# Two transformer layers on one core: order of row loads, weight fetches and leftover expert tiles in layer 0

## The chip, the cores and the metric

The kernel runs on one core of a Trainium2 chip. The metric is device time in microseconds for one execution of the whole program. Every engine (TensorE, VectorE, ScalarE, GpSimd, SyncE) runs its own list of instructions in order; semaphores tie the lists together. TensorE is called PE in the profile, VectorE DVE, ScalarE ACT, GpSimd POOL and SyncE SP.

## What is computed

Input x has 8 sequences of 512 tokens with 256 features, all in float32. Two layers follow one another; each is an attention part and an expert part, with a modulated layer norm before each and a gate after each. Only layer 0 is concerned here. Cut to what matters:

```python
# attention of layer 0: a delta rule, a serial scan over the 512 tokens
q = l2norm(silu(x @ Wq.T)); k = l2norm(silu(x @ Wk.T)); v = silu(x @ Wv.T)
beta = sigmoid(x @ Wbeta.T)                      # one per head, 16 heads of 16
def step(M, (q_t, k_t, v_t, b_t)):
    out_t = einsum('bnh,bnhd->bnd', q_t, M)
    delta = v_t - einsum('bnhd,bnd->bnh', M, k_t)
    return M + b_t * einsum('bnh,bnd->bnhd', k_t, delta), out_t
# experts of layer 0: each token goes to one of 8 experts
top = argmax(x @ gate_w.T + gate_b + expert_bias)
y   = relu(x @ w1[top] + b1[top]) @ w2[top] + b2[top]        # 256 -> 1024 -> 256
```

Layer 1 is a causal softmax attention with a relative bias, and a mixture of 8 dense experts.

## The kernel before, in words

The 512 tokens are cut into four chunks of 128 (`NT = 4`). For each chunk i three things are done.

**Front** (`front`): the tokens are loaded, normed (`stats`, L498 to L509 on ScalarE; `normal`, L525 and L526 on VectorE), turned (`turn`, L140 to L145), projected to q, k, v (`project`, L543 to L557), scaled (`roots`, `scales`, L668 to L676) and laid out by head (`heads`). `stats` of the last pair of sequences also clears the slot rows of its chunk in DRAM (L514, 1920 KB).

**Scan** (`scan`, L741 to L756): 128 steps of four VectorE instructions, each step needing the state of the step before.

**Follow** (`follow`): attention from the scan's deltas (`attend`; `deltas` L775, `turn` L786, `scores` L812, `weigh` L873, `project` L894 and L898, `rest` L929 to L934), routing (`route`), and the experts (`experts`). `attend` also loads the chunk's tokens once more for the residual (`tokens`, L768) on SyncE's queue, into eight buffers. Routing ends in the ranks' products on TensorE (L1074 to L1079); VectorE works out from them each token's slot and each slot tile's expert (L1087 to L1120, the last being `idx`). A chunk's 8 x 128 tokens are put by expert into 15 slot tiles of 128 rows (`NSLOT`), each tile belonging to one expert. Eight indirect DMAs on GpSimd's queue scatter the tokens to their rows in DRAM (`scatter`, L1126). Then for each slot tile j:

- its rows are loaded on SyncE's queue (L1162, two buffers), turned on TensorE (L1165) and copied by ScalarE (L1169); the code calls this `turn(j)`;
- first half: 32 products with w1 (L1190) and eight relus (L1199), which read the bias in the same weight tile;
- second half: 16 products with w2 (L1209), a copy (L1214), the bias add on GpSimd (L1215, which reads the second weight tile), and the store to DRAM on GpSimd's queue (L1216).

The weights of slot j come in two parts, fetch(j, 0) with w1 and b1 (1.05 MB) and fetch(j, 1) with w2 and b2 (1.18 MB), both indirect DMAs on GpSimd's queue (L1145). Each part has two buffers, so fetch(j, part) waits until slot j - 2 has done with its tile; the count runs on from one chunk to the next. After the slots, gathers (L1227) bring the results back to token order.

**What sets the order.** Each piece of front and follow has a place, a number. While chunk i + 1 is scanned, the pieces of chunk i's follow, of chunk i + 2's front and what was left of chunk i - 1's follow are sorted by place, and each is written out once the scan has come to the step of that number. A VectorE instruction of a piece is tied behind that scan step. On the other engines the place gives only priority: a scheduler orders each engine's list by priority and by when it expects an instruction's inputs. `tc.issue_after(ins)` ties every instruction written in its block that runs on the engine of `ins` behind `ins`. After the last scan there are no steps: the rest of chunk 2's slots, the attention of chunk 3 and its routing are written in order of place, then chunk 3's slots.

In `follow`, `late` says how many slots run during the scan, from place 68 on at `pace` places a slot; the others go to `starts` in the stretch after (during the next scan for chunks 0 and 1, after the last scan for chunk 2).

```python
            fetch(0, 0)
            with tc.issue_after(issued["fetch"]):
                scatter()
            with tc.issue_after(issued["scatter"]):
                fetch(0, 1)
                fetch(1, 0)
            yield
            turn(0)
```

Before the change GpSimd thus issues one fetch, the eight scatters, and then two fetches.

Of the kernel before, what the change touches and what calls it, by code (L numbers as in the profile page):

```python
# [19 lines left out]
P = 128  # L20
# [5 lines left out]
NT = S // P  # L26
# [37 lines left out]
def tile_two_layers(ctx: ExitStack, tc: tile.TileContext, t: dict, out: bass.AP):  # L64
    nc = tc.nc
# [212 lines left out]
    with ExitStack() as l0:  # L278
# [478 lines left out]

        def attend(i, qk, V, x1, norms):
# [6 lines left out]
            def tokens():  # L765
                for b in range(B):
                    x1.append(fp.tile([P, D], F32, tag="x1", name=f"x1_{i}_{b}", bufs=8))
                    nc.sync.dma_start(x1[b], t["x"][b, i * P : (i + 1) * P, :])  # L768
# [121 lines left out]
            def project(b):  # L890
# [6 lines left out]
                for g in range(2):  # L897
                    nc.tensor.matmul(  # L898
                        py[:, D : D + 1], sqT[:, g, :], cst[:, C_ONES : C_ONES + 1],
                        start=(g == 0), stop=(g == 1),  # L900
                    )
# [44 lines left out]
            pieces = [(0, deltas), (1, tokens)]  # L946
# [16 lines left out]


        DEPTH = (3, 3, 1, 1)

        issued = {}

        def route(i, h, norms):
# [31 lines left out]
            for half in range(2):  # L1001
# [3 lines left out]
                for n in range(5):  # L1005
                    b = 4 * half + n
# [72 lines left out]
            nc.tensor.matmul(  # L1079
# [3 lines left out]
            )  # L1083
# [51 lines left out]
        def experts(i, slot, idx, scatter):  # L1135
# [37 lines left out]
            fetch(0, 0)  # L1173
            with tc.issue_after(issued["fetch"]):
                scatter()
            with tc.issue_after(issued["scatter"]):
                fetch(0, 1)
                fetch(1, 0)
# [55 lines left out]
            if i == NT - 1:  # L1234
                rows = [w1["rows"][:, b * D : (b + 1) * D] for b in range(B)]
# [31 lines left out]
        def follow(i, qk, V):  # L1267


            x1, norms = [], []  # L1270
            _, pieces = attend(i, qk, V, x1, norms)
# [13 lines left out]
            def on():  # L1285
                next(work["experts"])

            pieces += [(34, begin), (42, more), (51, more), (57, more), (60, more), (62, settle)]

            late, pace, starts = {  # L1290
                NT - 1: (0, 4, [10 * j for j in range(NSLOT)]),
                NT - 2: (14, 4.2, [43]),
                NT - 3: (11, 4.6, [8, 22, 37, 47]),
            }.get(i, (11, 4.6, [8, 22, 37, 47]))
            rest = []
            for j in range(NSLOT):
                for half in range(2):
                    if j < late:
                        pieces.append((68 + pace * (j + half / 2), on))
                    else:  # L1300
                        rest.append((starts[j - late] + 3 * half, on))
# [52 lines left out]
        parts, pieces, later = front(0, 0)  # L1354
        run(pieces)
        rest, gathers = [], []
# [404 lines left out]
```

## Time and profile before

| | |
|---|---|
| median of 3 runs | 2216.25 us (2212.28 to 2221.45) |
| the profiled execution | 2215.8 us, its span 2214.1 us |
| scans 0 to 3 | 52 to 299, 299 to 570, 570 to 846, 846 to 1098 us |
| VectorE busy | 1580.6 us (71%) |
| TensorE busy | 1718.3 us (78%) |
| weight fetches | 120, on GpSimd's queue |
| slot rows loaded | 60 x 128 KB, on SyncE's queue |
| end of chunk 3's slots | 1344 us |
| TensorE's granted clock, mean | 0.874 |

All times are counted from the start of the span. A line of a timeline has the start, the time taken (both us), the engine, the line of the kernel, the operation, what is written and read, and a count; in brackets, how long the engine had been idle and what ended that. `PEld` is TensorE's loading of weights, `SPq` an issue on SyncE's queue. In the list of waits: who waited for whom, the total in us, how often, the longest. A line of windows gives the stretch, its length, the busy time of PE, PEld, DVE, ACT and POOL with instruction counts, TensorE's granted clock, the busy share of the 16 DMA engines and GB/s.

### The profile page before, as it was taken

The numbers are of one execution on the slowest core, as the hardware profiler recorded it, in microseconds if no ns is written. First come the engines' busy times: TensorE is split into PE (matmuls) and PEld (weight loads), VectorE is DVE, ScalarE is ACT, GpSimd is POOL, SyncE is SP. The second block draws the span as 40 slices with busy tenths as digits, with TensorE's granted clock in tenths as the row PEclk, the third lists the DMA queues.
The fourth block names the chain that finished last, engine by engine and source line by source line (L and its number), as shares of the span: only waits on it lengthen the run. The fifth ranks groups of instructions, "written<-read, shape, count | busy, mean of one in ns | idle before, by whom it ended". The sixth has DMA issues, their size and how long they took to land. (4 is left out here: it accounts for less than half of the span.)

```text
span 2214.1 us, 32513 instructions
## 1 busy us (share of the span) xinstructions
PE 1718.3 (78%) x10906; PEld 1196.4 (54%) x10906; DVE 1580.6 (71%) x4523; ACT 1081.1 (49%) x2674; POOL 642.1 (29%) x920
## 2 busy tenths in 40 slices
PE   5342056479686796839995898999999999999988
PEld 4221035259574695728874786555555555555544
DVE  5999998969989699899753004677676666676754
ACT  4253035555366553623342336886666574747421
POOL 1313013355254553543463643010111101010210
PEclk8666566689897898969997999999999999999998
DMA  5110000358103582128765883000101010000101
GB/s 165 49 50 5 0 1 11 99 209 313 33 13 108 198 311 72 38 90 303 234 110 153 272 275 72 1 20 8 27 13 25 13 22 13 22 20 6 23 17 12
DMA packets 88630, 189.58 MB, mean 86 GB/s; under 512 B 13688, under 2 KB 67104, under 8 KB 75664
## 3 DMA queue, kind: packets, MB, share of 16 engines
q0 software_dynamic: 33696, 137.43, 19.3%
q1 hardware_dynamic: 54768, 50.09, 7.9%
q8 instruction: 86, 1.41, 0.3%
q14 instruction: 80, 0.66, 0.1%
HBM read 175.10 MB, written 36.93 MB: 96 GB/s over the span
## 5 line engine op out<-in xcount | busy, mean ns | idle before, releaser
L1433 ACT ACTIVATE pr<-sc,low 128x384 f32<-128x384 f32 (+3 forms) x512 | 255.6, 556 | 196.3 <-DVE low L1428 193.2
L1428 DVE CUSTOM_DVE_ANT_0 sc<-ps,strips 128x384 f32<-128x384 f32 (+3 forms) x512 | 225.6, 486 | 87.2 <-PE ps L1419 55.6
L1190 PE MATMUL ps<-hTs,w 128*128 128x128 f32 x1920 | 239.4, 286 | 14.0 <-DMA w<-in_wrows,idx 9.0
L1190 PEld LDWEIGHTS ps<-hTs,w 128*128 128x128 f32 x1920 | 235.5, 201 | 21.4 <-issue 11.6
L745 DVE TENSOR_REDUCE state<-terms 128x16 f32<-128x272 f32 x512 | 227.3, 444 | 15.6
L756 DVE TENSOR_TENSOR state<-state,upd 128x256 f32<-128x256 f32 x511 | 222.2, 435 | 14.9
L1590 PE MATMUL ps<-ew,hTd 128*128 128x512 f32 x512 | 232.6, 608 | 0.0
L1209 PE MATMUL ps<-w,act 128*128 128x256 f32 x960 | 223.7, 387 | 6.5 <-DMA w<-in_wrows,idx 4.0
L741 DVE TENSOR_TENSOR terms<-state,K 128x256 f32<-128x256 f32 x512 | 216.3, 422 | 14.9
L751 DVE TENSOR_TENSOR upd<-K,state 128x256 f32<-128x256 f32 x511 | 214.4, 420 | 16.1
L1199 ACT ACTIVATE act<-ps,w 128x128 f32<-128x128 f32 x480 | 137.3, 370 | 135.4 <-PE ps L1190 122.2
L1445 PE MATMUL ps<-cst,pr 128*128 128x128 f32 x1280 | 189.9, 292 | 15.3 <-DVE low L1428 12.0
L1209 PEld LDWEIGHTS ps<-w,act 128*128 128x128 f32 x960 | 182.0, 195 | 31.4 <-issue 4.0
L1595 DVE SCALAR_TENSOR_TENSOR accd<-ps,wtd,accd 128x256 f32<-128x256 f32 x256 | 123.7, 483 | 100.7 <-PE ps L1590 86.6
L1445 PEld LDWEIGHTS ps<-cst,pr 128*128 128x128 f32 x1280 | 147.2, 147 | 84.8 <-DVE low L1428 24.1
L1599 POOL TENSOR_TENSOR accd<-accd,bc_g 128x256 f32<-128x256 f32 x28 | 20.4, 728 | 545.6 <-DVE accd L1595 545.6
L1145 POOL DMA_INDIRECT w<-in_wrows,idx x120 | 124.2, 1035 | 184.1 <-ACT act L1199 58.8
L1590 PEld LDWEIGHTS ps<-ew,hTd 128*128 128x128 f32 x512 | 96.3, 193 | 120.5 <-issue 106.4
L1419 PE MATMUL ps<-kT,qTc 32*128 32x128 f32 (+3 forms) x1024 | 132.1, 491 | 4.4 <-DVE low L1428 2.6
L1454 DVE COPY prT<-ps 128x512 f32<-128x512 f32 (+3 forms) x256 | 117.0, 484 | 8.9 <-PE ps L1445 8.5
L1452 ACT COPY prT<-ps 128x512 f32<-128x512 f32 (+3 forms) x256 | 98.9, 414 | 7.2 <-PE ps L1445 6.6
L1165 PE MATMUL ps<-cst,hslot 128*128 128x128 f32 x120 | 24.7, 290 | 98.2 <-DMA hslot<-hs 71.3
(296 smaller groups left out, 2956.3 us busy)
## 6 DMA issues: line engine op xcount, KB each, us to landing
hs<-zero SPq DMA_DIRECT2D x4, 1920.0 KB
hslot<-hs SPq DMA_DIRECT2D x60, 128.0 KB
ys<-ysb POOLq DMA_DIRECT2D x60, 128.0 KB
x<-in_x SPq DMA_DIRECT2D x32, 128.0 KB
strips<-strip_d SPq DMA_DIRECT2D x16, 256.0 KB
out<-accd POOLq DMA_DIRECT2D x32, 128.0 KB
wm<-in_wmod SPq DMA_DIRECT2D x4, 768.0 KB
xt<-in_x SPq DMA_DIRECT2D x12, 256.0 KB
```

What stands on the lines that cost most here:

```text
L741: nc.vector.tensor_mul(term[:, :, :HD], M, K[:, s, :].unsqueeze(1).to_broadcast([P, HD, HD]))
L745: nc.vector.tensor_reduce(delta, term, AX.X, ALU.add)
L751: nc.vector.tensor_mul(upd, K[:, s, :].unsqueeze(2).to_broadcast([P, HD, HD]), delta.unsqueeze(1).to_broadcast([P, HD, HD]),)
L756: yield nc.vector.tensor_sub(M, M, upd).ins
L1190: nc.tensor.matmul(ph[:, q * P : (q + 1) * P], w[:, k * FF + f * P : k * FF + (f + 1) * P], hT[:, k, :], start=(k == 0), stop=(k == 1),)
L1199: nc.scalar.activation(act[:, f, :], ph[:, q * P : (q + 1) * P], AF.Relu, bias=w[:, 2 * FF + f : 2 * FF + f + 1],)
L1209: nc.tensor.matmul(py[:, :D], act[:, f, :], w[:, f * D : (f + 1) * D], start=(f == 0), stop=(f == NFC - 1),)
L1419: made = nc.tensor.matmul(pscs[r][:, :W], qT[rows, g, o, i * P : (i + 1) * P], kT[rows, g, :W], start=True, stop=True,)
L1428: nc.vector.tensor_tensor_reduce(out=sc[:, :W], in0=pscs[r][:, :W], in1=strips[:, n, S - W :], scale=1.0, scalar=3.0e38, op0=ALU.add, op1= ...
L1433: nc.scalar.activation(pr, sc[:, :W], AF.Exp, bias=low, scale=-1.0)
L1445: nc.tensor.transpose(pt[:, (i - j) * P : (i - j + 1) * P], prs[r, i][:, j * P : (j + 1) * P], ident,)
L1590: nc.tensor.matmul(pe, hT[0][:, k, cols], ew[:, k, e : e + 2, :], start=(k == 0), stop=(k == 1),)
```

## The change

Four edits, all in layer 0.

1. `tokens`: the loads are tied behind the slot row that was issued last when the piece is written (`issued["rows"]`), if there is one. They are on the same queue.
2. `experts`: fetch(0, 0), fetch(0, 1) and fetch(1, 0) come first, then the eight scatters.
3. The first slot's place goes from 68 to 70. Chunk 2 runs 12 slots, not 14, during the last scan.
4. Slots left over: those at a place below 43 are written as before; one at 43 has its TensorE instructions tied behind the attention's last product written so far (L898), those at 61 behind the ranks' last product (L1079). For chunks 0 and 1 the four left go to 8, 22, 40, 61 (before: 8, 22, 37, 47); for chunk 2 three go to 43, 61 and 61.4 (before: one at 43).

```diff
             def tokens():
                 for b in range(B):
                     x1.append(fp.tile([P, D], F32, tag="x1", name=f"x1_{i}_{b}", bufs=8))
-                    nc.sync.dma_start(x1[b], t["x"][b, i * P : (i + 1) * P, :])
+                    with ExitStack() as order:
+                        if "rows" in issued:
+                            order.enter_context(tc.issue_after(issued["rows"]))
+                        nc.sync.dma_start(x1[b], t["x"][b, i * P : (i + 1) * P, :])
...
-            fetch(0, 0)
+            for j, part in ((0, 0), (0, 1), (1, 0)):
+                fetch(j, part)
             with tc.issue_after(issued["fetch"]):
                 scatter()
-            with tc.issue_after(issued["scatter"]):
-                fetch(0, 1)
-                fetch(1, 0)
             yield
             turn(0)
...
+            def behind(what):
+                with tc.issue_after(issued[what]):
+                    on()
+
             pieces += [(34, begin), (42, more), (51, more), (57, more), (60, more), (62, settle)]
 
             late, pace, starts = {
                 NT - 1: (0, 4, [10 * j for j in range(NSLOT)]),
-                NT - 2: (14, 4.2, [43]),
-                NT - 3: (11, 4.6, [8, 22, 37, 47]),
-            }.get(i, (11, 4.6, [8, 22, 37, 47]))
+                NT - 2: (12, 4.3, [43, 61, 61.4]),
+            }.get(i, (11, 4.6, [8, 22, 40, 61]))
             rest = []
             for j in range(NSLOT):
                 for half in range(2):
                     if j < late:
-                        pieces.append((68 + pace * (j + half / 2), on))
+                        pieces.append((70 + pace * (j + half / 2), on))
+                        continue
+                    place = starts[j - late]
+                    if i == NT - 1:
+                        rest.append((place + 3 * half, on))
+                    elif place < 43:
+                        rest.append((place + 3 * half, on))
                     else:
-                        rest.append((starts[j - late] + 3 * half, on))
+                        what = "ranks" if place > 60 else "attention"
+                        rest.append((place + 0.2 * half, lambda what=what: behind(what)))
```

The rest of the diff records `issued["attention"]` at L898 and `issued["ranks"]` at L1079, and moves `issued` and `DEPTH` up. Here `on` runs the next half of a slot, `begin` and `more` the stages of routing, `settle` the last stage with the fetches and scatters.

More of the change, by code (lines that the diff above doesn't have):

```diff
@@ L756, in scan @@
                 yield nc.vector.tensor_sub(M, M, upd).ins
+        DEPTH = (3, 3, 1, 1)
+        issued = {}
         def attend(i, qk, V, x1, norms):
@@ L897, in project @@
                 for g in range(2):
-                    nc.tensor.matmul(
+                    issued["attention"] = nc.tensor.matmul(
                         py[:, D : D + 1], sqT[:, g, :], cst[:, C_ONES : C_ONES + 1],
                         start=(g == 0), stop=(g == 1),
-                    )
+                    ).ins
                 h = b // 4
@@ L962, in attend @@
             return got, pieces
-        DEPTH = (3, 3, 1, 1)
-        issued = {}
         def route(i, h, norms):
@@ L1078, in route @@
             )
-            nc.tensor.matmul(
+            issued["ranks"] = nc.tensor.matmul(
                 pr[:, B * NE : B * NE + NE], count,
@@ L1082, in route @@
                 start=True, stop=True,
-            )
+            ).ins
             yield
```

## The prediction

> **What bounds the kernel now.** I read the page first: busy times and the 40 slices (55.4 us each), then the waits of VectorE, then the timelines of the engines around the two places where VectorE stands still.
>
> ```profile
> PE 1718.3 (78%) x10906; PEld 1196.4 (54%) x10906; DVE 1580.6 (71%) x4523; ACT 1081.1 (49%) x2674; POOL 642.1 (29%) x920
> DVE  5999998969989699899753004677676666676754
> ```
>
> No engine bounds the whole. VectorE is at 9 from slice 2 to slice 19: there run the four scans of layer 0, one instruction after the other, from 52 to 1098 us. Then come a stretch in which TensorE works off the last chunk (1098 to 1344 us) and layer 1, which the change does not touch. So the change is worth what it takes out of VectorE's stalls before 1098 us, plus what it takes out of the stretch up to 1344 us.
>
> The waits of VectorE within scans 1 and 2 (297 to 846 us):
>
> ```profile
> DVE rsa L525 <- ACT sda L509: 39.8, 4, 19.1
> ```
>
> Two of those four are 18.1 us (to 474.6) and 19.1 us (to 751.0); everything else in the scans is under 3 us each. Around the second, ScalarE, then SyncE's queue:
>
> ```profile
> 717.50 0.26 ACT L669 ACTIVATE beta<-beta 128x64 f32<-128x64 f32 x1
> 732.98 0.37 ACT L1169 COPY hTs<-ps 128x256 f32<-128x256 f32 x1 [15.22 <-PE ps L1165]
> ...
> 745.08 0.41 ACT L498 ACTIVATE ps<-xt 128x256 f32<-128x256 f32 x1
> ...
> 750.65 0.29 ACT L509 ACTIVATE sda<-mva,cst 128x2 f32<-128x2 f32 x1
> ```
> ```profile
> 715.86 5.39 SPq L768 DMA_DIRECT2D x<-in_x  x7
> 721.87 0.58 SPq L1162 DMA_DIRECT2D hslot<-hs  x2
> ```
> ```profile
> 712.00:722.00 10.00, 0.00 (x0) 0.00 (x0) 9.38 (x25) 5.69 (x9) 8.01 (x10) 0.61 0.94 327
> 722.00:732.00 10.00, 0.00 (x0) 0.00 (x0) 9.14 (x22) 0.00 (x0) 1.53 (x5) 0.50 0.85 326
> ```
>
> ScalarE stands 15.2 us at the copy of slot 0's turned rows; the statistics of the next chunk (L498, L509), which need nothing of slot 0, are queued behind that copy, and VectorE's L525 waits for them. The rows were asked for at 721.9 and reached TensorE at 732.3, 10.4 us later; seven token loads stand ahead of them in SyncE's queue. The last two columns of the windows: the 16 DMA engines are 94 and 85% busy, TensorE does nothing.
>
> The stretch after the scans:
>
> ```profile
> 1094.38 3.62 PE L1209 MATMUL ps<-w,act 128*128 128x256 f32 x16
> 1103.21 5.44 PE L1190 MATMUL ps<-hTs,w 128*128 128x128 f32 x32 [5.21 <-DMA w<-in_wrows,idx]
> ...
> 1112.16 1.96 PE L775 MATMUL ps<-cst,V 128*128 128x128 f32 x16
> ```
> ```profile
> 1188.10 0.54 PE L1079 MATMUL ps<-cst,count 64*128 64x8 f32 x2
> ...
> 1191.88 1.10 POOL L1145 DMA_INDIRECT w<-in_wrows,idx  x1 [9.86 <-DVE idx L1120]
> 1193.64 1.04 POOL L1126 DMA_INDIRECT hs<-h_last,slot  x1 [0.66 <-issue]
> ...
> 1202.66 0.97 POOL L1126 DMA_INDIRECT hs<-h_last,slot  x1 [0.30 <-issue]
> 1203.94 1.04 POOL L1145 DMA_INDIRECT w<-in_wrows,idx  x1 [0.30 <-issue]
> ...
> 1211.53 0.69 PE L1165 MATMUL ps<-cst,hslot 128*128 128x128 f32 x2 [22.89 <-DMA hslot<-hs]
> ```
>
> The scan's last copy (L747) ends at 1098.1, but chunk 2's slot 13 holds TensorE until 1112.2 before the last attention (L775) begins. From the ranks' products (end 1188.6) to slot 0's rows (1211.5) TensorE is empty for 22.9 us. Then 15 slots take 132 us.
>
> **What the Trainium skill says.** "DMA: Bandwidth & Descriptors", sections "Queues, rings and completion order" and "Issuing engines are not separate DMA queues": each DMA engine takes a ring in order and goes round-robin between rings, and all issuing engines share the same 16. The trace agrees: the rows take 10.4 us from issue to use behind tokens and weights, 8.0 in scan 3 (992.3 to 1000.3), 5.6 in the last stretch with no tokens (1205.9 to 1211.5). "Perfetto Trace Analysis", section "Sequencer Loop": an engine's queued instruction waits for its semaphores; here the 15.2 us with ready statistics behind it. "TensorE: Matmul & The Clock Gate", section "What's actually happening": an idle TensorE falls to half clock. The windows agree (0.50), and slot 0's 32 products take 5.4 to 6.0 us after a bubble, 3.7 otherwise.
>
> **The change part by part.**
>
> *Tokens behind rows.* 8 loads of 128 KB leave the space ahead of and beside slot 0's rows, in scans 1, 2 and 3. They go behind the slot row last issued (chunk 1's to about 553 us, chunk 3's to about 1080, ahead of the strips at 1087.7) and are first needed 25 steps into the next attention: nothing is late. The 1 MB beside the weights of slots 12 and 13 is covered by the 7 us that TensorE has to spare before 1098; gone, it would cost some 3 us. The rows save the 1.05 MB; the rows' own time goes from 10.4 towards 5.6, so 3 to 5 us.
>
> *Three fetches ahead of the eight scatters.* GpSimd issues a fetch in 1.3 us (1203.94, 1205.29), so the scatters start 2.6 us later. Where DMA is full (scans 1 and 2, 0.94 to 1.00 of 16 engines, the clearing of the next chunk's slot rows, 1.92 MB issued at 702.8, among it), their data also queue behind 1.18 + 1.05 MB, which at 327 GB/s is 6.8 us; 5.4 at the 0.41 MB per us that the packets reach at best. The scatters' packets ended about 717.3; so 722.7, 2 us to the semaphore, and about 4 us for the rows (only one fetch beside them): 728.7 against 732.3. **Minus 3 us** in scan 2; the same sum for scan 1 (scatters' packets end 442.5, rows 456.1) gives 2 to 3. In scan 3, with no clearing in the way, +2.6 and -2.5 cancel: 1000 us as before.
>
> *What this does to the stalls.* The ScalarE chain from rows to L509 is 18.7 us (732.3 to 751.0), of which 6.0 are slot 0's products at half clock. It moves with the rows: **-3 in each of scans 1 and 2, -6**. If the shift from place 68 to 70 and the later rows put the statistics ahead of the copy, the stall goes nearly whole (a rival below). I take -6, ends 0 and -30.
>
> *Slots moved within scans 2 and 3.* Slot 14 goes from place 47 to behind the ranks. Its 7.3 us of products (3.7 + 3.6) go where TensorE was idle (972.3 to 1000.3 in scan 3), and no longer delay the attention's last projection: VectorE's 0.9 us waits at 663, 666, 940, 942 us may go, **-2**. In scan 2 they lie ahead of the front's projections 2 and 3 (702 to 712), which may make L525 at 715 wait up to 4 us; that only takes from the longer stall after it, since that one ends by the rows. Cover gone, it costs 4.
>
> *Twelve slots, not fourteen, in scan 3.* Slot 11 ends at 1090.8, before the scan (1098.1), so the last attention starts then and not at 1112.2: **-14.0**. Slot 12 takes slot 14's old place (1172.0 to 1179.2, while ScalarE and VectorE finish the rows): 0. The ranks end at R = 1174.6.
>
> *Slots 13 and 14 behind the ranks.* 14.6 us of products in a bubble of 22.9: hidden themselves. But weights have two buffers per part. Before, fetch(0,0) went at R + 3.2, when the indices were there. Now it waits for slot 13's activations (R + 3.7 + 1.5 = 5.2), fetch(0,1) for slot 13's bias add (R + 7.4 + 2.5 = 9.9), fetch(1,0) for slot 14's activations (R + 11 + 1.5 = 12.5), and the scatters queue behind it: R + 14.1, not R + 5.0. **+9.1**, plus 1.6 if slot 14's bias add and store (0.7 + 0.6 and gaps) go between. Against it, the rows have one fetch beside them, not three: 5.6 becomes about 4, **-1.5**. Rows at R + 30.5 against R + 22.9. So slot 0 starts -14.0 + 7.6 = **-6.4**. The 132 us that follow are tied to TensorE and to two weight buffers, each fetch waiting for a slot to end: they shift, 0.
>
> Sum: -6 - 2 - 6.4 = **-14.4**. The profiled execution took 2215.8 (span 2214.1 and 1.7 around it): 2201.4. The median of the runs is 0.4 above; I say **2201**.
>
> **Rivals.**
> 1. *The stalls go.* ScalarE gets the statistics ahead of the copy. For: ScalarE is empty for 15 us, the inputs were loaded at 702.3, and the tail of the schedule already put L668 (place 79) ahead of the copy (68). Against: L498 did stay behind. Of 37.2 us some 8 stay (half-clock products, square roots): -29 - 2 - 6.4 = -37, **2178**.
> 2. *The gain is eaten.* Rows come no earlier and the store goes ahead of the scatters: 0 - 0 - 4.8: **2211**, no difference.
> 3. *Slower: the scatters drown in the weights.* Tokens did not hold up the rows, so the 5.4 us of weights come in full on both stalls (+10.8); and in the last stretch the weights of slot 14 or the scatters run as late (+5.4 over +9.1 + 1.6 - 14): +2. **2229**. It decides if rows in scan 2 arrive after 732.3. Against: SyncE's tokens stand before and among the rows, and DMA needs the same bytes less 1 MB.
>
> **How the numbers follow.** Forecast 0.47, rival 1 0.28, rival 2 0.16, rival 3 0.09. A measurement of this kernel tells some 0.5% (11 us) from no change: 2205 and 2227. Of the forecast's 0.47 about 0.36 lies below 2205. Faster 0.64, same 0.28, slower 0.08. The range takes in rival 2 and all but a third of rival 1, leaving that and rival 3 out: 2174 to 2218.
>
> **What would show it.** Attention (L775) at the end of scan 3, not 14 us later; slots 13 and 14 in the bubble; scatters about 14 us after the ranks there; 128 KB row loads in scans 1 and 2 landing in 4 to 7 us with no token loads near; the two L525 waits at 15 us each. Wrong if those waits are gone (rival 1), or above 19 (rival 3), or if GpSimd issues the scatters within 6 us of the ranks or more than 18 after.

## The result and the profile after

| | before | after |
|---|---|---|
| median of 8 runs each, same chip | 2219.8 us (2212.28 to 2227.97) | 2202.53 us (2196.75 to 2209.05) |
| ratio after to before, 95% interval | | 0.9923 (0.9902 to 0.9945) |
| the profiled execution, its span | 2215.8, 2214.1 us | 2209.05, 2207.3 us |

The changed kernel is faster by 0.77%, some 17 us. Its profiled execution is the longest of its eight, so its trace shows less of the gain than the runs do. After's line numbers are 2 to 9 higher than before's; in the experiments they differ by some more. L1169 is now the turning of a slot's rows, L1173 their copy, L1192 and L1211 the two halves of a slot, L1130 the scatters, L1149 the fetches, L1166 the row loads, L943 the stores of x.

The page's busy times and VectorE's 40 slices:

```profile
PE 1730.0 (78%) x10906; PEld 1208.3 (55%) x10906; DVE 1582.4 (72%) x4523; ACT 1080.0 (49%) x2674; POOL 640.6 (29%) x920
DVE  5999999979989799899751004677676666666654
```

The instruction counts are those of before and each engine's busy time is within 1% of it: the work is the same, only its order differs.

VectorE's waits between 297 and 846 us, in after (who waited for whom, total, times, longest):

```profile
DVE rsa L525 <- ACT sda L509: 19.4, 3, 10.5
```

It was 39.8 us, the longest 19.1. The two long stalls, 18.1 and 19.1 us, are now 10.5 and 8.6.

ScalarE around the second of them:

```profile
708.40 1.07 ACT L140 ACTIVATE xna<-xt,offa,rsa 128x256 f32<-128x256 f32 x2
...
721.56 0.37 ACT L1173 COPY hTs<-ps 128x256 f32<-128x256 f32 x1 [9.82 <-PE ps L1169]
...
729.13 0.40 ACT L498 ACTIVATE ps<-xt 128x256 f32<-128x256 f32 x1
...
736.43 0.30 ACT L509 ACTIVATE sda<-mva,cst 128x2 f32<-128x2 f32 x1
```

The copy still stands ahead of the statistics, but it waits 9.8 us and not 15.2, and from the copy to the end of L509 it takes 15.2 us and not 18.0: the norm of the next sequence (L140) has moved ahead of the copy.

The stretch after the scans, TensorE first, then GpSimd:

```profile
1074.23 3.62 PE L1211 MATMUL ps<-w,act 128*128 128x256 f32 x16
1078.77 2.07 PE L784 MATMUL ps<-cst,V 128*128 128x128 f32 x16 [0.92 <-DVE V L747]
...
1148.15 0.69 PE L1169 MATMUL ps<-cst,hslot 128*128 128x128 f32 x2 [5.11 <-DMA hslot<-hs]
1148.63 5.98 PE L1211 MATMUL ps<-w,act 128*128 128x256 f32 x16
...
1163.32 5.61 PE L1192 MATMUL ps<-hTs,w 128*128 128x128 f32 x32
...
1198.28 0.69 PE L1169 MATMUL ps<-cst,hslot 128*128 128x128 f32 x2 [18.65 <-DMA hslot<-hs]
```
```profile
1170.38 1.00 POOL L1149 DMA_INDIRECT w<-in_wrows,idx  x1 [12.24 <-ACT hTs L1173]
...
1178.23 0.99 POOL L1149 DMA_INDIRECT w<-in_wrows,idx  x1 [2.12 <-ACT act L1201]
...
1181.05 1.03 POOL L1130 DMA_INDIRECT hs<-h_last,slot  x1 [0.17 <-issue]
1182.09 0.60 POOL L1218 DMA_DIRECT2D ys<-ysb  x1
...
1190.62 0.96 POOL L1130 DMA_INDIRECT hs<-h_last,slot  x1 [0.30 <-issue]
```

The last attention (L784) begins right behind the scan, 33.4 us earlier than before. From there the lead shrinks: 25.2 us at the ranks' products (R, 1163.4), 13.2 at slot 0's rows (1198.3), 8.3 at the end of chunk 3's slots (1335.8).

### The profile page after: what moved, and what is told of

The parts are those of the page before. It is cut to its first block, busy times and chain, and to the rows that moved or that the text cites. A ratio compares the mean times of both kernels' runs of the same rounds, so it can differ in the third digit from the quotient of the medians.

```text
span 2207.3 us, 32493 instructions
## 1 busy us (share of the span) xinstructions
PE 1730.0 (78%) x10906; PEld 1208.3 (55%) x10906; DVE 1582.4 (72%) x4523; ACT 1080.0 (49%) x2674; POOL 640.6 (29%) x920
## 5 line engine op out<-in xcount | busy, mean ns | idle before, releaser
L1447 ACT ACTIVATE pr<-sc,low 128x384 f32<-128x384 f32 (+3 forms) x512 | 255.7, 556 | 197.2 <-DVE low L1442 193.8
L1192 PE MATMUL ps<-hTs,w 128*128 128x128 f32 x1920 | 243.8, 289 | 12.6 <-DMA w<-in_wrows,idx 7.8
L1192 PEld LDWEIGHTS ps<-hTs,w 128*128 128x128 f32 x1920 | 239.4, 204 | 19.9 <-issue 10.9
L1211 PE MATMUL ps<-w,act 128*128 128x256 f32 x960 | 226.4, 391 | 11.5 <-DMA w<-in_wrows,idx 8.9
L756 DVE TENSOR_TENSOR state<-state,upd 128x256 f32<-128x256 f32 x511 | 222.7, 436 | 15.0
L1201 ACT ACTIVATE act<-ps,w 128x128 f32<-128x128 f32 x480 | 136.6, 372 | 148.2 <-PE ps L1192 139.5
L1211 PEld LDWEIGHTS ps<-w,act 128*128 128x128 f32 x960 | 183.8, 197 | 37.9 <-issue 7.6
L1459 PE MATMUL ps<-cst,pr 128*128 128x128 f32 x1280 | 191.7, 295 | 14.5 <-DVE low L1442 11.6
L1149 POOL DMA_INDIRECT w<-in_wrows,idx x120 | 124.3, 1036 | 186.8 <-ACT hTs L1173 78.3
L1480 PE MATMUL ps<-prT,v 128*32 128x512 f32 (+3 forms) x1024 | 96.6, 448 | 0.0
```

The source lines that it names most:

```text
L756: yield nc.vector.tensor_sub(M, M, upd).ins
L1192: nc.tensor.matmul(ph[:, q * P : (q + 1) * P], w[:, k * FF + f * P : k * FF + (f + 1) * P], hT[:, k, :], start=(k == 0), stop=(k == 1),)
L1211: nc.tensor.matmul(py[:, :D], act[:, f, :], w[:, f * D : (f + 1) * D], start=(f == 0), stop=(f == NFC - 1),)
L1447: nc.scalar.activation(pr, sc[:, :W], AF.Exp, bias=low, scale=-1.0)
L1459: nc.tensor.transpose(pt[:, (i - j) * P : (i - j + 1) * P], prs[r, i][:, j * P : (j + 1) * P], ident,)
L1480: nc.tensor.matmul(yT[32 * r : 32 * r + 32, j * P :], v[:, j, 4 * c + r, :], prTs[r][:, :W], start=(j == 0), stop=(j == NT - 1),)
```

## The experiments

Each kernel was timed in five rounds beside the kernel before. They ran in three groups of four, in the order of the table, on three chips, where the kernel before had medians of 2220.5, 2218.7 and 2229.1 us; so kernels are compared by their ratios to it. Scan lengths are from the first to the last state update (L756); stage times come from each kernel's one profiled execution, so a few us between two kernels are no finding by themselves. A first overview, in us:

| kernel | ratio to before (95%) | two stalls | scans 1 + 2 | scan 3's end to R | R to slot 0's rows |
|---|---|---|---|---|---|
| before | 1 | 18.1, 19.1 | 542.9 | 92.3 | 22.9 |
| after | 0.9923 (0.9902 to 0.9945) | 10.5, 8.6 | 522.4 | 86.5 | 34.9 |
| tokens alone | 0.9924 (0.9891 to 0.9956) | 11.8, 12.2 | 530.8 | 84.1 | 22.7 |
| fetches ahead alone | 0.9985 (0.9964 to 1.0006) | 10.0, 12.2 | 525.5 | 99.6 | 24.4 |
| places alone | 0.9967 (0.9949 to 0.9986) | 15.7, 17.4 | 534.4 | 89.2 | 28.0 |
| after, last chunk's fetches as before | 0.9872 (0.9832 to 0.9911) | 8.3, 7.4 | 518.5 | 81.2 | 27.9 |
| after, chunk 2's slots as before | 0.9893 (0.9870 to 0.9916) | 9.1, 9.4 | 520.7 | 88.2 | 24.3 |
| after, slot 13's row sooner | 0.9910 (0.9883 to 0.9937) | 8.1, 7.6 | 517.0 | 87.2 | 35.9 |
| the same, scatters first in last chunk ("both") | 0.9799 (0.9773 to 0.9825) | 8.1, 7.6 | 518.0 | 81.6 | 19.3 |
| after, slot 0 at place 74 | 0.9911 (0.9884 to 0.9938) | 3.9, 2.4 | 510.7 | 87.6 | 34.9 |
| both, scatters first in all chunks | 0.9764 (0.9731 to 0.9797) | 3.7, 4.2 | 512.8 | 84.4 | 19.4 |
| the same, slot 0 at place 74 | 0.9724 (0.9690 to 0.9757) | 1.3, 2.4 | 506.7 | 80.6 | 19.6 |
| both, tokens as before | 0.9821 (0.9788 to 0.9855) | 10.5, 10.2 | 522.8 | 83.2 | 19.4 |
| both, places as before | 0.9834 (0.9799 to 0.9869) | 8.6, 9.6 | 522.2 | 85.8 | 18.9 |

### One edit at a time

**Tokens alone** (edit 1; fetch order and places as before):

```diff
-            for j, part in ((0, 0), (0, 1), (1, 0)):
-                fetch(j, part)
+            fetch(0, 0)
             with tc.issue_after(issued["fetch"]):
                 scatter()
+            with tc.issue_after(issued["scatter"]):
+                fetch(0, 1)
+                fetch(1, 0)
```

(and edits 3 and 4 undone; this and the next two diffs are against after.)

> The kernel before with the first edit alone: token loads behind the slot row last issued. Theory A (the scans' gain comes mostly from ScalarE's and VectorE's order around the copy of slot 0's rows, which the places set, and only a little from earlier rows): the order stays as before, the rows of slot 0 reach TensorE about 3 us sooner after the indices in scans 1 and 2, both long L525 waits go from 18 and 19 to 15 and 16 us, the last stretch is unchanged: 6 us less than before, ratio 0.997. Theory B (earlier rows alone made the gain): 15 to 20 us less, ratio 0.992.

Measured: 0.9924, theory B's value; 0.997 is outside the interval. Moving the eight loads of each chunk gives, alone, as much as the four edits together. Slot 0's rows are copied 21.8 and 22.1 us behind the index (the start of `idx`, 430.0 and 699.1) instead of 28.4 and 29.3, and VectorE comes to L525 after as many scan steps as before (79). In scan 2, SyncE's queue (the first of four row loads) and TensorE:

```profile
713.65 19.34 SPq L1166 DMA_DIRECT2D hslot<-hs  x4
```
```profile
720.50 0.66 PE L1169 MATMUL ps<-cst,hslot 128*128 128x128 f32 x2 [12.47 <-DMA hslot<-hs]
```

About half of the gain is SyncE's own queue: it issues the row load 13.8 and 14.5 us behind the index, before 17.6 and 18.2, since seven token loads no longer stand ahead of it (the scatters' last packets end 13.3 and 13.9 us behind the index, before 14.1 in both). The other half is the transfer, from issue to TensorE 7.3 and 6.8 us instead of 10.1 and 10.4. This half agrees with the Trainium skill's statement that the issuing engines share the same 16 DMA engines ("DMA: Bandwidth & Descriptors", "Issuing engines are not separate DMA queues"); but one engine issues both tokens and rows, so the run doesn't test sharing between issuers.

The last stretch gains too. TensorE no longer waits 5.2 us for slot 13's weights, the attention begins 7.2 us behind the last state update and not 15.9, and R to slot 0 stays at 22.7 us. Why those weights are in time stays open.

**Fetches ahead alone** (edit 2; `tokens` as before, edits 3 and 4 undone):

```diff
-                    with ExitStack() as order:
-                        if "rows" in issued:
-                            order.enter_context(tc.issue_after(issued["rows"]))
-                        nc.sync.dma_start(x1[b], t["x"][b, i * P : (i + 1) * P, :])
+                    nc.sync.dma_start(x1[b], t["x"][b, i * P : (i + 1) * P, :])
```

> The kernel before with the second edit alone: three fetches ahead of the eight scatters, in all chunks. Theory A: rows 0 to 3 us later in scans 1 and 2 (5.4 us of weights ahead of the scatters, the same bytes gone behind them), L525 waits 18 to 21 us; in the last stretch no slot holds the weight buffers, so scatters start 2.6 us later and slot 0 one to two us later after the ranks (24 to 25 us, not 22.9): within 4 us of the kernel before, ratio 0.999 to 1.002. Theory B: rows 3 us sooner even without the token edit, 6 us less, ratio 0.997.

Measured: 0.9985, no difference that this measurement tells from none. Theory A's ratio fits and its waits don't (10.0 and 12.2 us, not 18 to 21); theory B's 0.997 lies within the interval too, but its rows 3 us sooner are 0.7 and 1.0. Scans 1 and 2 do gain, -17.4 us together: VectorE reaches L525 after 82 scan steps, not 79, with its other work done. The stretch after takes it back: scan 3's end to R +7.3 (the attention begins 3.5 us later behind the scan, as slot 13 still waits 5.2 us for weights, and takes 3.7 us longer), R to slot 0 +1.5, the 15 slots +6.2 (138.8 against 132.6).

**Places alone** (edits 3 and 4; `tokens` and the fetch order as before):

```diff
-                    with ExitStack() as order:
-                        if "rows" in issued:
-                            order.enter_context(tc.issue_after(issued["rows"]))
-                        nc.sync.dma_start(x1[b], t["x"][b, i * P : (i + 1) * P, :])
+                    nc.sync.dma_start(x1[b], t["x"][b, i * P : (i + 1) * P, :])
...
-            for j, part in ((0, 0), (0, 1), (1, 0)):
-                fetch(j, part)
+            fetch(0, 0)
             with tc.issue_after(issued["fetch"]):
                 scatter()
+            with tc.issue_after(issued["scatter"]):
+                fetch(0, 1)
+                fetch(1, 0)
```

> The kernel before with the third and fourth edits alone: first slot at place 70, leftover slots moved and tied. Theory A: in scans 1 and 2 the long L525 waits shrink by about 6 us each, since one turn goes ahead of the copy and L525 stands two scan steps later; rows arrive as before. In the last stretch the attention begins 14 us sooner relative to the scan's start, slot 12 loses about 7 us to the row load of slot 13, and slot 0 comes some 28 us after the ranks (only the first fetch waits for a slot): net -1 to -3 there. Together 14 us less, ratio 0.994. Theory B: the scans as before, ratio 0.999.

Measured: 0.9967, between the theories and outside the value of each. The stalls shrink by 2.4 and 1.7 us only, not by 6: L525 comes after 78 and 79 scan steps, no later than before. The attention begins 6.0 us behind the last state update and not 15.9, but R comes 23 us behind the attention's last product and not 16.5, slot 0's rows at R + 28.0, and the 15 slots take 141.6 us. So this edit's cost lies in the last stretch.

### Where the lead goes after the scans

**The last chunk's fetches as before** (the rest as after):

```diff
-            for j, part in ((0, 0), (0, 1), (1, 0)):
-                fetch(j, part)
-            with tc.issue_after(issued["fetch"]):
-                scatter()
+            if i < NT - 1:
+                for j, part in ((0, 0), (0, 1), (1, 0)):
+                    fetch(j, part)
+                with tc.issue_after(issued["fetch"]):
+                    scatter()
+            else:
+                fetch(0, 0)
+                with tc.issue_after(issued["fetch"]):
+                    scatter()
+                with tc.issue_after(issued["scatter"]):
+                    fetch(0, 1)
+                    fetch(1, 0)
```

> The kernel after, but in the last chunk one fetch, the eight scatters, then two fetches, as before the change. Theory A (the scatters stand behind fetches that wait for slots 13 and 14): scatters begin at ranks + 9 us, not + 17.7, slot 0 reaches TensorE at ranks + 28, not + 34.9, and all after it shifts: 6 to 8 us less than the kernel after, ratio to the kernel before about 0.989. Rival (the start of slot 0 is set by the transfers' own time or the stage's length is set by DMA anyway): same as after, 0.992.

Measured: 0.9872, theory A's side; the rival's 0.992 is outside the interval, which overlaps after's a little. The first scatter leaves at R + 10.5 and not R + 17.7, and slot 0's rows come at R + 27.9 and not R + 34.9. These 7.0 us are two fetches that wait for slots 13 and 14 to give weight buffers up, with the scatters queued behind them on GpSimd.

**Chunk 2's slots as before** (14 in the scan, one in the attention; the rest as after, also the pace of 4.3 and the tie of the slot at 43):

```diff
-                NT - 2: (12, 4.3, [43, 61, 61.4]),
+                NT - 2: (14, 4.3, [43]),
```

> The changed kernel with only the slots of chunk 2 placed as in the kernel before: 14 slots inside scan 3 at a pace of 4.2 to 4.3 steps and the last one in the attention, instead of 12 inside and three behind. Theory A (placing fewer slots in scan 3 is what starts the attention 14 us sooner, and the row of slot 13 that then stands behind the strips' loads gives half of it back): scan 3's last slot runs past the scan again, the attention starts about 12 to 16 us after the scan's last subtraction instead of 2, but the ranks end about 16.5 us after the attention instead of 24.0; on balance 5 to 7 us lost at the ranks, R to slot 0 still 35: 0.995 of the kernel before. Theory B (the tokens loaded late already free the slots of scan 3, so that 14 of them end only 6 us behind it, as in the run with the tokens alone): attention 6 to 8 us behind the scan, ranks 16.5 behind the attention, so nothing is lost against the changed kernel: 0.991 to 0.992.

Measured: 0.9893, theory B's side (0.995 is outside the interval), and the interval overlaps after's. The attention begins 11.7 us behind the last state update (after: 1.9), R comes 16.7 us behind the attention (after: 24.0), and slot 0's rows at R + 24.3. The last neither theory had: with no slot left over, the fetches find their buffers free and the scatters start at R + 7.7. So in the kernel as changed, the 9.8 us that the attention gains cost 7.3 before R and 10.6 behind it.

**Slot 13's row sooner.** `load(j)` is the row load cut out of `turn(j)`:

```diff
                 turn(j + 1)
+                if i == NT - 2 and j == 11:
+                    load(13)
                 w = ws[j, 1]
```

> The changed kernel with one row load moved: slot 13 of chunk 2 has its row load issued together with the second half of slot 11, so that it stands on SyncE's queue right behind the row load of slot 12 and ahead of the loads and stores of the attention. Theory A (TensorE waits 5.1 us for that row between the attention and the ranks, and then runs slot 12's second half at half clock): the ranks end 16 to 17 us behind the attention instead of 24.0, everything behind them comes 7 us earlier: 0.989 of the kernel before. Theory B (the ranks wait for the layer norm and router of the last half, which take those 24 us anyway): the ranks stay at 23 to 24 us, 0.992 as the changed kernel.

Measured: 0.9910, 0.13% under after with intervals that overlap: no more than the trace says. Its TensorE between attention and ranks (L1201 and L1222 are the halves):

```profile
1137.34 5.24 PE L1201 MATMUL ps<-hTs,w 128*128 128x128 f32 x32
...
1142.63 3.62 PE L1222 MATMUL ps<-w,act 128*128 128x256 f32 x16
1148.16 0.93 PE L1018 MATMUL ps<-cst,xnf 128*128 128x128 f32 x4 [1.91 <-ACT xnf L1013]
```

The 5.1 us wait for the row is gone, but R is 21.0 us behind the attention, not 16 to 17: slot 12's first half runs slower here (5.2 us against 3.8), and then the norm of the last half, which in after had been done during the wait, is what TensorE waits for. Of theory A's 7.5 us only 3.0 come back.

**Both: scatters first in the last chunk, and slot 13's row sooner:**

```diff
-            for j, part in ((0, 0), (0, 1), (1, 0)):
-                fetch(j, part)
-            with tc.issue_after(issued["fetch"]):
+            if i < NT - 1:
+                for j, part in ((0, 0), (0, 1), (1, 0)):
+                    fetch(j, part)
+                with tc.issue_after(issued["fetch"]):
+                    scatter()
+            else:
                 scatter()
+                with tc.issue_after(issued["scatter"]):
+                    for j, part in ((0, 0), (0, 1), (1, 0)):
+                        fetch(j, part)
```

> The changed kernel with the row load of slot 13 moved as in the run above, and with the last chunk's eight scatters ahead of its three fetches of weights (in the other chunks the fetches stay ahead). Theory A (what the last stretch lost is the 7.5 us of that row and the 12 us that the scatters stand behind fetches that wait for slots 12 and 13 to give their weight buffers up): ranks 16.5 us behind the attention, slot 0's rows on TensorE at about R + 20 instead of R + 34.9, then 3 to 6 us of it given back as waits for the first weights, fetched 12 us later than the scatters: 15 to 20 us less than the changed kernel, 0.984 to 0.986 of the kernel before. Theory B (the weights, not the rows, decide when slot 0 can run: fetched behind the scatters, they come as much later as the rows come sooner): slot 0's rows sooner but its first products at R + 34 again; only the row's 7 us are gained: 0.989.

Measured: 0.9799, below what theory A gave. (The weight buffers that the fetches wait for are those of slots 13 and 14.) TensorE from R on (L1207 is the first half here, L1178 the turning of the rows), then GpSimd:

```profile
1154.27 5.96 PE L1207 MATMUL ps<-hTs,w 128*128 128x128 f32 x32
...
1173.61 0.44 PE L1178 MATMUL ps<-cst,hslot 128*128 128x128 f32 x2 [2.67 <-DMA hslot<-hs]
1174.51 3.84 PE L1207 MATMUL ps<-hTs,w 128*128 128x128 f32 x32 [0.46 <-ACT hTs L1182]
```
```profile
1156.88 1.03 POOL L1130 DMA_INDIRECT hs<-h_last,slot  x1 [9.14 <-DVE idx L1124]
...
1165.90 0.97 POOL L1130 DMA_INDIRECT hs<-h_last,slot  x1 [0.30 <-issue]
1167.17 1.04 POOL L1149 DMA_INDIRECT w<-in_wrows,idx  x1 [0.30 <-ACT act L1216]
```

The scatters start at R + 2.6, the rows are on TensorE at R + 19.3, and slots 13 and 14 fill all but 2.7 us of the way there (after: 18.7 us idle). Slot 0's first product waits for no weights, though fetch(0, 0) left only 7.3 us ahead of it: theory B is wrong. The 15 slots take 134.1 us (after: 137.5).

### What is left of the stalls

**Slot 0 at place 74** in scans 1 and 2 (after with only this):

```diff
-                        pieces.append((70 + pace * (j + half / 2), on))
+                        pieces.append(((70 if i == NT - 2 else 74) + pace * (j + half / 2), on))
```

> The changed kernel with the first slot placed at step 74 instead of 70 in scans 1 and 2 (later slots keep their spacing behind it); the list of ScalarE then has the layer norm's and the states' work of scan step 80 ahead of the copy of slot 0's turned rows. Theory A (the remaining stall of 10.5 and 8.6 us of the scan is the ScalarE operations behind that copy, which waits for the rows; put ahead of it they cost the scan nothing): the stall at that subtraction goes to under 2 us in both scans, scans 1 and 2 take 250 to 253 us instead of 258.6 and 263.8 if the slots still fit, so 0.985 to 0.987 of the kernel before. Theory B (the stall is only moved: another operation of VectorE that needs ScalarE stands behind the copy, or the slots pushed later run past the scan's end): scan lengths as in the changed kernel to within 3 us, 0.992 or a little more.

Measured: 0.9911, theory B's value; the time doesn't tell it from after, though the scans are shorter than theory B had them. ScalarE in scan 2:

```profile
713.07 0.39 ACT L498 ACTIVATE ps<-xt 128x256 f32<-128x256 f32 x1
...
720.20 0.29 ACT L509 ACTIVATE sda<-mva,cst 128x2 f32<-128x2 f32 x1
...
722.67 0.37 ACT L1173 COPY hTs<-ps 128x256 f32<-128x256 f32 x1
```

The statistics now stand ahead of the copy, as the prediction's first rival had it, and no part of what is left of the stall comes from the rows. Still 3.9 and 2.4 us remain, not under 2, and the scans take 255.0 and 255.7, not 250 to 253: by this timeline L509 now ends when the front's own projections and square roots let it, which no run here took away. The scans' 11.7 us against after's profile may be too many by some 4, since the same instructions in "both" take 4.4 us less than after's. At the end of the 15 slots this profile, of the shortest of its six executions, is 8.6 us ahead of after's, of the longest of its eight; the medians show 0.12%.

**Scatters first in all chunks** (both, with the new order in every chunk):

```diff
-            if i < NT - 1:
-                for j, part in ((0, 0), (0, 1), (1, 0)):
-                    fetch(j, part)
-                with tc.issue_after(issued["fetch"]):
-                    scatter()
-            else:
-                scatter()
-                with tc.issue_after(issued["scatter"]):
-                    for j, part in ((0, 0), (0, 1), (1, 0)):
-                        fetch(j, part)
+            scatter()
+            with tc.issue_after(issued["scatter"]):
+                for j, part in ((0, 0), (0, 1), (1, 0)):
+                    fetch(j, part)
```

> The kernel of the run e8_both (row load of slot 13 moved, last chunk's scatters ahead of its three fetches) with the scatters ahead of the three fetches in the other three chunks too. Theory A (also inside the scans the rows are late because the scatters wait behind fetches: idx to the last scatter takes 16.5 to 18.3 us in the changed kernel where 9 us of issue would do): slot 0's rows are copied 21 to 23 us behind the index instead of 27.3 and 26.6, the stalls at the statistics of scan step 80 fall from 10.5 and 8.6 us to 3 to 6, scans 1 and 2 lose 3 to 5 us each: 0.975 to 0.977 of the kernel before. Theory B (in the scans the weights are then late instead, so slot 0's products and with them the slots' pace do not move): rows sooner, scan lengths as in e8_both (257.3 and 260.7) to within 2 us: 0.980.

Measured: 0.9764, theory A's value, though the interval overlaps that of "both". The rows are copied 17.5 and 19.0 us behind the index, sooner than theory A had it, and slot 0's products follow them with no wait for weights. The stalls fall by 4.4 and 3.4 us against "both", the scans by 3.7 and 1.5, the second less than theory A's 3 to 5. Rows that come 8 us sooner gain no more in part because L525 is back at 78 and 79 scan steps ("both": 81), so VectorE reaches it sooner too. Its VectorE waits between 300 and 850 us, against the 19.4 of after:

```profile
DVE rsa L525 <- ACT sda L509: 9.2, 3, 4.2
```

GpSimd in after shows what the fetches ahead cost inside a scan:

```profile
700.46 1.04 POOL L1149 DMA_INDIRECT w<-in_wrows,idx  x1 [0.30 <-issue]
701.80 1.04 POOL L1130 DMA_INDIRECT hs<-x,slot  x1 [0.30 <-issue]
...
709.48 0.97 POOL L1130 DMA_INDIRECT hs<-x,slot  x1 [1.51 <-DMA w<-in_wrows,idx]
```

The scatters start 6.8 us behind the index (695.0), and the issue of two of them (the second is left out here) waits 1.5 and 0.8 us, by the trace until weights have landed.

**The same with slot 0 at place 74:**

```diff
-                        pieces.append((70 + pace * (j + half / 2), on))
+                        pieces.append(((70 if i == NT - 2 else 74) + pace * (j + half / 2), on))
```

> The run before's kernel (scatters first in all chunks, row of slot 13 moved) with the first slot placed at step 74 in scans 1 and 2, which puts the statistics of scan step 80 ahead of the copy on ScalarE's list. Theory A: what is left of the two stalls goes (under 1 us each; with the fetches first, place 74 left 3.9 and 2.4), scans 1 and 2 take 250 to 253 us: 0.973 to 0.975 of the kernel before. Theory B (the later slots run past the end of scans 1 and 2, or wait elsewhere; with the fetches first place 74 moved the median by no more than 0.1%): as the run before to within 0.2%.

Measured: 0.9724, the best of all, 2.8% under the kernel before and some 2% under the kernel as changed. The stalls are 1.3 and 2.4 us, not under 1 each; the scans take 253.1 and 253.6. Its interval overlaps that of the run before, and in its profile the 15 slots take 142.6 us (run before: 135.0), so that place 74 adds 0.4% is not shown.

### Leaving one edit out of the mended kernel

**Both, tokens as before** (against "both"):

```diff
-                    with ExitStack() as order:
-                        if "rows" in issued:
-                            order.enter_context(tc.issue_after(issued["rows"]))
-                        nc.sync.dma_start(x1[b], t["x"][b, i * P : (i + 1) * P, :])
+                    nc.sync.dma_start(x1[b], t["x"][b, i * P : (i + 1) * P, :])
```

> The kernel of the run e8_both with the tokens loaded as in the kernel before (not behind the slots' rows). Theory A (the token edit alone gave 0.76%, by rows that come 7 us sooner beside a free DMA, and this adds to the rest): copy of slot 0's rows 29 us or more behind the index, stalls of 13 to 17 us in scans 1 and 2, 0.986 to 0.988 of the kernel before. Theory B (what the token edit gains in the scans the places gain too, since they queue the statistics later; the edits overlap): 0.981 to 0.983.

Measured: 0.9821, within theory B's range; theory A's is outside the interval. Stalls of 10.5 and 10.2 us, 2.4 and 2.6 more than in "both".

**Both, places as before**, against "both" (without the earlier load for slot 13, which is not late there):

```diff
-                NT - 2: (12, 4.3, [43, 61, 61.4]),
-            }.get(i, (11, 4.6, [8, 22, 40, 61]))
+                NT - 2: (14, 4.2, [43]),
+                NT - 3: (11, 4.6, [8, 22, 37, 47]),
+            }.get(i, (11, 4.6, [8, 22, 37, 47]))
...
-                        pieces.append((70 + pace * (j + half / 2), on))
+                        pieces.append((68 + pace * (j + half / 2), on))
```

> The token edit, and the last chunk's scatters ahead of its three fetches, with the places of the slots as in the kernel before (fetches ahead of the scatters in the other chunks). Theory A (the places are worth most of a per cent: they start the attention right at the end of scan 3 and queue step 80's statistics ahead): attention 7 to 12 us behind the scan's end, ranks 16.5 us behind the attention, slot 0's rows at R + 20, 0.988 to 0.990 of the kernel before. Theory B (with the tokens late and the scatters first the places no longer matter): 0.980 to 0.983.

Measured: 0.9834, at the edge of B's range and off A's; the interval overlaps that of "both" (0.9799). The attention begins 8.7 us behind the last state update.

The edits overlap. Alone, the tokens give 0.76%; beside the other edits, 0.22%, and the difference to "both" is within the intervals. Each of the first two edits takes 6 to 8 us off each stall by itself; all four together take 7.6 and 10.5.

## Why the prediction was right, and where it was not

The number was right: forecast 2201, measured 2202.53; of the rivals none fits as a whole (2178, 2211, 2229). That it came so near is in part luck: the sum of -14.4 is near the 17 us measured because several errors of its terms cancel. By its steps, from the profiled executions:

| step | predicted | found |
|---|---|---|
| scans 0 to 3 (last state update) | -8 | -19.4 |
| attention begins at the scan's end | -14.0 | -14.0 |
| attention's own length | 0 | +0.7 |
| attention's end to R | 0 | +7.5 |
| R to slot 0's rows | +7.6 | +12.0 |
| the 15 slots | 0 | +4.9 |
| layer 1 | 0 | +1.5 |
| sum | -14.4 | -6.8 |

The sum found compares two executions: before's took 4.0 us less than its median, after's 6.5 us more, which is the gap between -6.8 and the medians' -17. Four kernels of the table share its instructions through scans 1 and 2 or all but the last chunk (last chunk's fetches as before, chunk 2 as before, slot 13's row, both); they end scan 3 at 1071.3 to 1073.9 us, not 1076.9, which is 3 to 6 of the 10 us. Two waits of VectorE at the attention's last projection (L934) are 4.1 and 2.3 us in after's profile and 1.0 us each in those four, which is 4.5 us of it. So the "-2" for slot 14's products shows in those four, as the waits at that place were 3.6 us in all in the kernel before; in after's own profile it does not.

**The stalls: mechanism half right, size wrong.** VectorE's slices, read as nines from 2 to 19, have two sixes, the 9th and the 14th: they hold the two stalls, and in after they are sevens. "It moves with the rows: -3 in each of scans 1 and 2." In scan 2 the rows did move by about that: on TensorE 25.9 us behind the index, before 28.6. What the step left out is the rest of the chain. From rows to L525 it takes 15.9 us, not 18.7, since L140 and L145 of the next sequence went ahead of the copy; and VectorE comes to L525 5.9 us later in its scan, with two more scan steps (3.7 us) and other work behind it, which was time for the chain to run.

So the stall's end came 4.6 us sooner in the scan (-2.7 rows, -2.8 chain, +0.9 index), and another 6.0 us of work no longer follow it: -10.6 in scan 2. In scan 1 the rows came only 1.1 us sooner behind the index; the stall's end came 4.5 us sooner and VectorE 3.1 us later.

That VectorE comes later goes with the second edit, to which the prediction gave no such effect: with slot 0 at place 68 or 70, L525 comes after 78 or 79 scan steps in every kernel with at most one fetch ahead of the scatters in the scans, and after 81 or 82 in every kernel with three. Presumably the scheduler then expects slot 0's rows, and with them L525's inputs, later; that is inferred, not tested. It is no case of the first rival: L498 stayed behind the copy. Place 74 shows what that rival would have been, 2 to 4 us of stall left.

The reason given for the rows, "SyncE's tokens stand before and among the rows", is shown by the tokens alone, and was sized too low: 7 us, not 3 to 5. The transfer's own gain was about as forecast (2.8 and 3.6 us); left out were the 3.8 and 3.7 us by which SyncE issues the row load sooner. The "2 us to the semaphore" are too many: in after SyncE issues the row load 0.4 and 0.7 us behind the scatters' last packet. What hid the 7 us is the other half of the sum: the fetches ahead of the scatters delay the rows by some 4 us within the scans (25.5 and 26.3 us behind the index with tokens late and fetches ahead at the old places, 21.8 and 22.1 with tokens late only), and by 7 to 8 against scatters first (25.6 and 26.5 in "both", 17.5 and 19.0).

**The attention** begins where the prediction put it. The reason given, twelve slots in scan 3 instead of fourteen, is shown in part: with 14 back it begins 11.7 us behind the last state update, not 1.9. But the places alone leave 6.0 us (TensorE waits 4.0 us for slot 11's weights there), and the tokens alone already turn 15.9 into 7.2. So the -14.0 belongs to both edits, and the prediction gave the tokens nothing of it.

**Slot 12 in slot 14's old place, "0".** This step failed. Its second half is written behind `turn(13)`, and `turn` also issues the row load. In after, SyncE issues that load between the stores of x:

```profile
1142.13 0.87 SPq L943 DMA_DIRECT2D x<-x  x2
1143.10 0.40 SPq L1166 DMA_DIRECT2D hslot<-hs  x1
```

The row lands 5 us later, TensorE stands for 5.1 us, and the 16 products after it take 6.0 us instead of 3.6. The prediction had not followed this one DMA past SyncE's queue. Slot 14 in that place had no next slot to turn. Moving the load brought back 3 of the 7.5 us; most of the rest is slot 12's first half, 1.4 us slower there, and the 1.9 us wait for the norm, which the wait for the row had covered.

**The scatters behind the fetches** was the right mechanism, mis-sized: first scatter at R + 17.7, not R + 14.1. Slot 13's first half took 5.6 us, not 3.7, at a mean granted clock of 0.74 (so fetch(0, 0) went at R + 7.0, not R + 5.2), and slot 14's bias add went ahead of the scatters, its store behind the first of them. Two experiments confirm the mechanism: with two fetches put back behind the scatters the rows come 7.0 us sooner; with all three behind, 16.6 us sooner than in the kernel that differs in this alone ("slot 13's row sooner", R + 35.9 to R + 19.3).

**"They shift, 0"** for the 15 slots missed 4.9 us: TensorE's waits for weights there were 7.8 us before and 12.5 after. That the two buffers make this stage depend on when the first fetches go is argued, not shown; in the profiles of all kernels it took 132.6 to 142.6 us.

**The signs.** Of those that the prediction named, the attention at the scan's end, slots 13 and 14 in the bubble and rows that land in 4 to 7 us (5.2 and 4.8 to TensorE) came. The two waits of 15 us each did not (10.5 and 8.6), and the scatters at R + 17.7 were just short of the 18 that it called wrong.

**Still open.** Why the fetches ahead, alone, lose 6 us in the 15 slots when their order in the last chunk costs only 1.5 us up to slot 0 ("chunk 2's slots as before", whose fetches also go ahead with their buffers free, takes 139.6 us there); and how much the places are worth in the mended kernel (0.35% by the medians, not told from nothing).

## What to carry to other kernels

When an instruction is queued behind others on an in-order queue, count what those others wait for, not what they cost to issue: three fetches of 1.3 us each held eight scatters back for 15 us because each had a buffer to wait for. Put the small transfers that the next stage's first instruction needs ahead of the large ones, and move bulk loads that are needed late behind them; here that took 6.6 to 7.2 us from one 128 KB load's way. When a forecast comes out right, look at its terms all the same: here a gain of twice the expected size hid losses that edits of a few lines removed for another 1.2 to 2%.

## What the hardware showed that was not expected

Layer 1, which no kernel here touches, took between 861.8 and 875.1 us in the profiled executions. The windows of the kernel with slot 13's row sooner and of "both, places as before", from the end of the slots to the end of the span (start and end, length, busy time of PE, PEld, DVE, ACT and POOL, granted clock, DMA share, GB/s):

```profile
1329.20:2191.00 861.80, 819.42 (x4767) 451.29 (x4765) 570.68 (x1980) 508.63 (x1125) 110.06 (x141) 0.97 0.10 20
```
```profile
1312.90:2188.00 875.10, 833.21 (x4766) 462.35 (x4764) 571.74 (x1980) 509.95 (x1125) 110.24 (x141) 0.96 0.10 20
```

The instructions are the same and VectorE's time agrees within 0.2%; TensorE is busy 13.8 us longer at a granted clock of 0.96 instead of 0.97. These 13 us are 0.6% of the span, in a stage that no edit touches. So the spans of two profiles can't rank kernels that are 0.5% apart; the stages before it, or the medians, have to be read.
